# Summing GNN messages in spans of 32 nodes on quarters of TensorE's columns instead of 64 nodes on halves

## The chip, the core and the metric

The kernel runs on one core of a Trainium2 chip. The metric is the device time of one execution in microseconds (us). A core has TensorE (PE, with its weight loads shown as PEld), VectorE (DVE), ScalarE (ACT), GpSimd (POOL), SyncE (SP) and 16 DMA engines; all of them run on their own and wait for one another through semaphores.

## The reference: what is computed

The program is a stack of four blocks on 1250 nodes of 512 features, all in float32: graph attention, a mixture of 64 experts, a message-passing layer with a GRU cell, and a spline network. The edges are 20,000 edges of a random graph in both directions with 1250 self-loops, 21,250 in all, sorted by destination `dst`. The change lies in the message-passing layer:

```
m_in = concatenate([h[src], edge_attr], axis=1)          # 21250 x (512 + 128)
m    = relu(m_in @ W1.T + b1) @ W2.T + b2
agg  = segment_sum(m, dst, num_segments=1250)            # sums per destination node
gi   = agg @ W_ih.T + b_ih
gh   = h @ W_hh.T + b_hh
...                                                      # GRU cell, batch norm, h + bn
```

Since W2 is linear, the kernel sums relu(...) per node first (the tensor `rT`, features by nodes) and multiplies by W2 behind the sum.

## The kernel before

The work runs in stages: attention, routing, shared experts and experts (to about 1050 us of the trace), a stage that forms `ptab` = h @ W1[:512].T + b1 per node and writes it to HBM, the message loop (L900 to L938), and then the GRU cells and the spline network. A scheduler puts each engine's instructions into an order when the program is built: it goes by the order of the program, and an instruction that isn't ready by its estimate is passed by later ones that are. `tc.issue_after(x)` makes what is issued within it come behind x on x's engine. Within an engine the order is then fixed, and an instruction that waits holds up all behind it.

Edges are cut into 167 tiles of 128 (`ET`). As they are sorted by destination, a tile's edges lead to few nodes: about 7.5 per tile. The loop takes 8 tiles (a group) at a time, in two windows of `WT` = 4 tiles, each with 64 nodes (`WN`) around the place where its edges are expected.

- `eat` (L907): one DMA on SP's queue brings the edge features of 8 tiles, 512 KB, two buffers.
- `at` (L912): DVE writes, per tile, a 128 x 64 matrix of zeros and ones: row e, column n is 1 if edge e leads to the window's node n. It comes from `dnear`, the destination plus 1, or 0 if it isn't near the place where it is expected.
- `messages` (L885) takes a pair of tiles, one of each window: two gathers on POOL (`hg`, L203, called by L891: 128 rows of 2 KB from `ptab`, four pairs of buffers), two matmuls into `pm` (L892: 128 edges x 512), DVE's addition m = pm + hg (L894) and ACT's relu on m (L895). Behind some of them ACT's queue issues loads of later weights (`load_late`).
- `ps` (L921): for each of the two tiles a matmul with `at` as the weights: 64 columns of the array, so 64 rows of the PSUM tile `ps`. The two windows of the pair lie in its two halves. Four pairs are accumulated.
- ACT copies `ps` to `s` (L924), TensorE transposes it in four pieces to `pt` (L935), and DVE adds each window's 64 columns of it to `rT` at the window's place (L938): two additions a group.

The core of it, with the placing by window:

```
for h, i in enumerate(js):
    nc.tensor.matmul(ps[h * WN:(h + 1) * WN], at[:, i], m[:, h], start=j == 0,
                     stop=j == WT - 1 or i == n - 1)
...
for c in range(DC):
    nc.tensor.transpose(pt[:, c], s[:, c * P:(c + 1) * P], ident)
for i in range(2):
    r = rT[:, :, window(w + i):window(w + i) + WN]
    nc.vector.tensor_add(r, r, pt[:, :, i * WN:(i + 1) * WN])
```

In groups 5, 6 and 7 the node degrees are also turned into a row (`cnt`, L929 to L931). Edges that aren't near their place are counted once at the start (`far_i`); behind the loop, all engines read the count and skip a slow path (L941) if it is zero, as it is here.

Other lines that the text speaks of: L399 is the router's matmul (64 columns), L579 to L590 the shared experts, with DVE's product L583 and sum L590; L619 a comparison of 128 x 128 by DVE; L628 the load of the experts' token lists on SP and L710 the loads of the experts' weights (SP, 1.5 MB each); L682 to L691 a check of the experts' loads; L726 the experts' first matmuls, which for small experts put four tiles of 32 tokens side by side on quarters of the columns (128*32); L720, L736 and L743 the experts' transposes and second matmuls; L832 an addition of 128 x 512 by DVE; L1027 the first matmul behind the loop.

Of the kernel before, what the change touches and what calls it, by code (L numbers as in the profile page):

```python
# [10 lines left out]
F32 = mybir.dt.float32  # L11
# [3 lines left out]
I32 = mybir.dt.int32  # L15
U32 = mybir.dt.uint32
AF = mybir.ActivationFunctionType
OP = mybir.AluOpType
AX = mybir.AxisListType
# [3 lines left out]
P = 128  # L23
N = 1250
NT = 10
NP = NT * P
LAST = N - (NT - 1) * P
D = 512
# [23 lines left out]
HB = P // 2  # L52
WT, WN = 4, 64
NWIN = -(-ET // WT)


def window(w):

    return max(0, min(NP - WN, round((w + 0.5) * WT * P * N / E - WN / 2)))

# [19 lines left out]
def gnn_ffn_kernel(ctx: ExitStack, tc: tile.TileContext, a: dict, out: bass.AP):  # L80
# [57 lines left out]
    hT = const.tile([P, DC, NP], F32, name="hT")  # L138
    deg = const.tile([P, NT], F32, name="deg")

    def row(start, n):
# [452 lines left out]
    with tc.tile_pool(name="moe", bufs=1, side="right") as mw, tc.tile_pool(name="moe_w", bufs=6) as ew:  # L594
        with tc.tile_pool(name="moe_s", bufs=1) as keep, \
# [83 lines left out]


            cap = keep.tile([P, 1], F32, name="cap")
            nc.vector.tensor_scalar(cap, rank, float(TWOS), None, op0=OP.is_ge)  # L682
# [165 lines left out]
    with ExitStack() as kan:  # L848
# [11 lines left out]
        if True:  # L860
# [22 lines left out]
            nc.vector.memset(rT, 0.0)  # L883

            def messages(work, psum, parts, ahead, late=lambda i: None):  # L885

# [3 lines left out]
                for i, (t, eat_t) in enumerate(parts):  # L890
                    gather(hg[:, i], ptab, srci[:, t:t + 1])  # L891
                    nc.tensor.matmul(pm[:, i], eat_t, w1e, start=True, stop=True)  # L892
                m = work.tile([P, 2, D], F32, name="m")
# [5 lines left out]

            with tc.tile_pool(name="msg_e", bufs=3) as work, \  # L900
                    tc.tile_pool(name="msg_c", bufs=2) as chunks, \
                    tc.tile_pool(name="msg_ep", bufs=2, space=PSUM) as psum:
                for w in range(0, NWIN, 2):
                    t0 = w * WT
                    n = min(2 * WT, ET - t0)
                    eat = chunks.tile([P, 2 * WT * P], F32, name="eat")
                    nc.sync.dma_start(out=eat[:, :n * P], in_=a["edge"][:, t0 * P:(t0 + n) * P])  # L907
                    at = work.tile([P, 2 * WT, WN], F32, name="at", bufs=2)
                    for i in range(2):
                        ts = slice(i * WT, min((i + 1) * WT, n))  # L910
                        k = ts.stop - ts.start
                        nc.vector.scalar_tensor_tensor(  # L912
                            at[:, ts], iot[:, None, :WN].to_broadcast([P, k, WN]), float(window(w + i) + 1),
                            dnear[:, t0 + ts.start:t0 + ts.stop, None].to_broadcast([P, k, WN]),
                            op0=OP.add, op1=OP.is_equal)
                    ps = psum.tile([P, D], F32, name="ps", bufs=2)
                    for j in range(WT):
                        js = [i for i in (j, j + WT) if i < n]
                        m = messages(work, psum, [(t0 + i, eat[:, i * P:(i + 1) * P]) for i in js], 4, load_late)
                        for h, i in enumerate(js):  # L920
                            nc.tensor.matmul(ps[h * WN:(h + 1) * WN], at[:, i], m[:, h], start=j == 0,  # L921
                                             stop=j == WT - 1 or i == n - 1)
                    s = work.tile([P, D], F32, name="s", bufs=2)
                    nc.scalar.activation(s, ps, AF.Copy)  # L924
                    if w in (10, 12, 14):
                        c0, m = CHUNKS[w // 2 - 5]
                        pc = psum.tile([1, 512], F32, name="pt")
                        for j in range(m // P):
                            nc.tensor.matmul(pc[:, j * P:(j + 1) * P], deg[:, c0 // P + j:c0 // P + j + 1],  # L929
                                             ident, start=True, stop=True)  # L930
                        nc.scalar.activation(cnt[:, c0:c0 + m], pc[:, :m], AF.Copy)  # L931

                    pt = psum.tile([P, DC, P], F32, name="pt")
                    for c in range(DC):
                        nc.tensor.transpose(pt[:, c], s[:, c * P:(c + 1) * P], ident)  # L935
                    for i in range(2):
                        r = rT[:, :, window(w + i):window(w + i) + WN]
                        nc.vector.tensor_add(r, r, pt[:, :, i * WN:(i + 1) * WN])  # L938

            far = nc.values_load(far_i[:, :], min_val=0, max_val=P * ET)  # L940
            with tc.If(far):  # L941
                with tc.tile_pool(name="far_k", bufs=1) as keep, \
                        tc.tile_pool(name="far_w", bufs=2) as work, \
                        tc.tile_pool(name="far_q", bufs=2, space=PSUM) as psum:
                    sums = keep.tile([P, NT, D], F32, name="sums")
                    nc.vector.memset(sums, 0.0)
                    for t in range(ET):
                        eat = work.tile([P, P], F32, name="eatf")
                        nc.sync.dma_start(out=eat, in_=a["edge"][:, t * P:(t + 1) * P])
                        m = messages(work, psum, [(t, eat)], 2)[:, 0]  # L950
                        for j in range(NT):
                            at = work.tile([P, P], F32, name="at")
                            nc.vector.tensor_scalar(at, iot, float(j * P), dres[:, t:t + 1],
                                                    op0=OP.add, op1=OP.is_equal)
# [385 lines left out]
```

## Time and profile before

| | us |
|---|---|
| median of 8 runs | 1990.03 (1986.88 to 1992.84) |
| profiled execution | 1993.95, span of its instructions 1992.2 |
| granted TensorE clock, mean of the span | 0.969 of full |
| message loop, first pm (1111.49) to the first matmul behind it (1388.35) | 276.9 |

In the lines of the profile, PE is matmuls, PEld weight loads, and L912 is line 912 of the kernel. A group line has the line, engine and operation, output<-inputs by the program's names, the form (for TensorE weights as rows*columns, then the data that is streamed), the count, then busy time and mean ns of one (busy time counts what overlaps once), and then the idle time of the engine just before, with what ended it. A timeline line has start, duration, engine, line and operation; neighbours of one kind are put together (x4). Matmuls are pipelined, so the duration of one is longer than the distance to the next.

### The profile page before, as it was taken

What the parts mean: (1) busy time and instruction counts of PE and PEld (TensorE: products, weight loads), DVE (VectorE), ACT (ScalarE), POOL (GpSimd) and SP (SyncE); (2) the same over time, 40 slices, a digit from 0 to 9 for tenths busy, and PEclk for the clock granted to TensorE, in tenths of its full rate; (3) what the DMA queues carried; (4) which work ended last, traced back from release to release, by engine and by line L of the source; (5) the groups of instructions that cost most, each with busy time, mean ns of one, the idle gap of its engine ahead of it and who ended that gap; (6) DMA issues with size and microseconds to landing.
All of it is one profiled execution on the core that took longest, in us unless ns stands there. A gap on an engine that the chain in (4) does not pass through costs nothing. (4 is left out here: it accounts for less than half of the span.)

```text
span 1992.2 us, 20446 instructions
## 1 busy us (share of the span) xinstructions
PE 1861.2 (93%) x7391; PEld 896.1 (45%) x7391; DVE 1034.3 (52%) x1740; ACT 757.5 (38%) x1193; POOL 440.8 (22%) x421
## 2 busy tenths in 40 slices
PE   6999998785999999999989799998999999998989
PEld 4673232242544444444434233332446866665633
DVE  8675958263111111111137254554234988799994
ACT  3215653231012222222222134333014886787772
POOL 0000002225034444444420365663000000000000
PEclk9999999786999999999999899999999999999999
DMA  8000000002579899898962577774010000000000
GB/s 305 4 1 2 1 22 1 1 22 75 208 205 304 272 311 307 248 299 298 298 188 85 161 225 237 248 248 139 24 71 0 1 32 32 32 11 1 11 10 22
DMA packets 68257, 247.14 MB, mean 124 GB/s; under 512 B 11872, under 2 KB 14560, under 8 KB 59044
## 3 DMA queue, kind: packets, MB, share of 16 engines
q1 hardware_dynamic: 29810, 147.56, 19.7%
q0 software_dynamic: 32656, 83.97, 16.3%
q10 hardware_dynamic: 5666, 14.05, 2.0%
q8 instruction: 65, 1.06, 0.2%
q14 instruction: 60, 0.49, 0.1%
HBM read 210.15 MB, written 35.39 MB: 123 GB/s over the span
## 5 line engine op out<-in xcount | busy, mean ns | idle before, releaser
L726 PE MATMUL pg<-w,xT 128*128 128x512 f32 (+4 forms) x752 | 274.8, 595 | 2.0 <-DMA w<-in_experts 1.5
L730 DVE TENSOR_TENSOR gs<-gs,pg 128x256 f32<-128x256 f32 (+2 forms) x76 | 31.9, 420 | 388.1 <-ACT gs L729 388.1
L203 POOL DMA_INDIRECT hg<-ptab,srci x167 | 158.1, 947 | 189.9 <-DVE at L912 91.1
L726 PEld LDWEIGHTS pg<-w,xT 128*128 128x128 f32 (+4 forms) x752 | 105.4, 164 | 158.5 <-issue 156.6
L892 PE MATMUL pm<-w1e,eat 128*128 128x512 f32 x334 | 170.4, 625 | 6.6 <-DVE m L894 5.8
L749 POOL DMA_INDIRECT acc<-y,goal x94 | 140.6, 1495 | 156.2 <-ACT y L747 134.4
L743 PE MATMUL py<-w,gT 128*128 128x512 f32 (+4 forms) x376 | 149.4, 611 | 9.6 <-ACT gT L738 3.3
L894 DVE TENSOR_TENSOR m<-pm,hg 128x1024 f32<-128x1024 f32 x84 | 102.3, 1218 | 103.0 <-PE pm L892 81.9
L1176 PE MATMUL pk<-basis,w1s 128*128 128x256 f32 x640 | 150.6, 381 | 4.3 <-DVE basis L1158 4.3
L1199 PE MATMUL py<-block,basis 128*128 128x512 f32 x320 | 141.6, 603 | 9.3 <-DVE basis L1158 9.3
L481 DVE SCALAR_TENSOR_TENSOR wt<-ex,cnts 128x1024 f32<-128x1024 f32 (+1 forms) x120 | 119.7, 1039 | 51.0 <-ACT ex L479 32.7
L479 ACT ACTIVATE ex<-ps 128x1024 f32<-128x1024 f32 (+1 forms) x120 | 101.3, 882 | 109.6 <-PE ps L474 70.2
L895 ACT ACTIVATE m<-m 128x1024 f32<-128x1024 f32 x84 | 88.2, 1050 | 141.9 <-DVE m L894 121.6
L1176 PEld LDWEIGHTS pk<-basis,w1s 128*128 128x128 f32 x640 | 119.9, 190 | 42.7 <-issue 14.6
L1131 ACT ACTIVATE sq<-held,negk 128x512 f32<-128x512 f32 x180 | 127.3, 709 | 24.3 <-DVE cube L1135 24.2
L1135 DVE SCALAR_TENSOR_TENSOR cube<-held,knots,sq 128x512 f32<-128x512 f32 x180 | 134.1, 747 | 4.4 <-ACT sq L1131 4.1
L747 ACT ACTIVATE y<-py,gate 128x512 f32<-128x512 f32 (+2 forms) x76 | 52.2, 686 | 160.6 <-PE py L743 120.4
L729 ACT ACTIVATE gs<-pg 128x256 f32<-128x256 f32 (+2 forms) x76 | 29.1, 383 | 219.7 <-PE pg L726 219.7
L203 POOL DMA_INDIRECT xg<-xtab,tok x76 | 75.0, 987 | 156.3 <-PE pt L720 120.1
L892 PEld LDWEIGHTS pm<-w1e,eat 128*128 128x128 f32 x334 | 56.0, 191 | 103.5 <-issue 90.8
L1199 PEld LDWEIGHTS py<-block,basis 128*128 128x128 f32 x320 | 61.6, 194 | 86.2 <-issue 71.7
L1142 ACT ACTIVATE right<-cube 128x512 f32<-128x512 f32 x135 | 84.0, 622 | 39.9 <-DVE cube L1135 35.9
(266 smaller groups left out, 2775.3 us busy)
## 6 DMA issues: line engine op xcount, KB each, us to landing
w<-in_experts SPq DMA_DIRECT2D x64, 1536.0 KB
eat<-in_edge SPq DMA_DIRECT2D x20, 512.0 KB
acc<-zero SPq DMA_DIRECT2D x33, 256.0 KB
part<-acc SPq DMA_DIRECT2D x30, 256.0 KB
block<-in_w SPq DMA_DIRECT2D x3, 1536.0 KB
w1s<-in_w1s ACTq DMA_DIRECT2D x4, 1024.0 KB
block<-in_Wih ACTq DMA_DIRECT2D x4, 768.0 KB
block<-in_Whh ACTq DMA_DIRECT2D x4, 768.0 KB
```

What stands on the lines that cost most here:

```text
L203: nc.gpsimd.indirect_dma_start(out=dst, out_offset=None, in_=table, in_offset=IndirectOffsetOnAxis(ap=at, axis=0))
L479: nc.scalar.activation(ex[:, :, :n], p[:, :, :n], AF.Exp, scale=DK ** -0.5)
L481: nc.vector.scalar_tensor_tensor(wt[:, :, :n], ex[:, :, :n], HUGE, cnts[:, b, None, n0:n0 + n].to_broadcast([P, 2, n]), op0=OP.min, op1=OP ...
L726: nc.tensor.matmul(ph[p0:p0 + n], xT[:, c, p0:p0 + n], weights[r][:, c:2 * DC:DC], start=c == 0, stop=c == DC - 1)
L743: nc.tensor.matmul(py[p0:p0 + n], gT[:, f, p0:p0 + n], weights[r][:, k:k + 2].rearrange("p a b -> p (a b)"), start=f == 0, stop=f == 1)
L749: nc.gpsimd.indirect_dma_start(out=next(turn), out_offset=IndirectOffsetOnAxis(ap=self.goal[:n, r, h:h + 1], axis=0), in_=y[p0:p0 + n], in ...
L892: nc.tensor.matmul(pm[:, i], eat_t, w1e, start=True, stop=True)
L894: nc.vector.tensor_add(m[:, :k], pm[:, :k], hg[:, :k])
L1131: nc.scalar.activation(self.sq[k], self.x, AF.Square, bias=negk[:, k:k + 1])
L1135: nc.vector.scalar_tensor_tensor(self.cube[k], self.x, knots[:, k:k + 1], self.sq.pop(k), op0=OP.subtract, op1=OP.mult)
L1176: nc.tensor.matmul(pk[o], w[:, o * P:(o + 1) * P], b[:, c], start=half == 0 and g == 8 and c == 0, stop=half == 1 and g == 7 and c == 1)
L1199: nc.tensor.matmul(py[m], b[:, c, m * P:(m + 1) * P], w, start=g == 8 and c == 0, stop=g == 7 and c == 1)
```

## The change

Windows become shorter and narrower: `WT` = 2 tiles and `WN` = 32 nodes, four of them (`WG`) in a group of 8 tiles; there are 21 groups as before. A window no longer lies where its edges are expected but begins at the destination of its first edge (`head`). For that, all partitions get row 0 of `dst` by one DMA on SP, and DVE works out, once and ahead of the experts, for each edge its place in its window plus 1, or 0 where it has none (`inwin`), how many edges have none (`out_i`), and for each of the 128 rows of `ps` the node to which it belongs (`aim`). On these inputs the destinations within 256 neighbouring edges lie at most 17 apart.

In the loop, a step now takes four tiles, one of each window: two calls of `messages` as before, and then four matmuls of 32 columns, into the four quarters of `ps`. The sums of a step are held back until the next step's pm matmuls are issued, and the copy of `ps` and what follows it too. The rows of `ps` are no longer at fixed nodes, and two windows can have the same node, so the transposes become true matmuls with a matrix of zeros and ones, `to` (row p, column n is 1 if row p of `ps` belongs to node n of the group's 128), which transposes, places and adds up in one; DVE then adds 128 columns to `rT` in one instruction. DVE writes `to` once a group and `at` in one instruction instead of two; `at` has three buffers instead of two, m four instead of three. The slow path tests `out_i`. `dres` and `far_i` are still used by the attention stage.

```diff
-WT, WN = 4, 64
-NWIN = -(-ET // WT)
+WT, WN, WG = 2, 32, 4
+NGRP = -(-ET // (WT * WG))
...
+            head_i = keep.tile([P, ET], I32, name="head_i")
+            d0 = a["dst"]
+            nc.sync.dma_start(out=head_i,
+                              in_=bass.AP(tensor=d0.tensor, offset=d0.offset, ap=[[0, P], [1, ET]]))
+            head = keep.tile([P, NGRP, WG], F32, name="head")
+            nc.vector.tensor_copy(head.rearrange("p g q -> p (g q)"), head_i[:, ::WT])
...
+            nc.vector.memset(inwin, -1.0)
+            nc.vector.tensor_sub(inwin[:, :whole], dstf[:, :whole * WT].rearrange("p (w i) -> p w i", i=WT),
+                                 heads[:, :whole, None].to_broadcast([P, whole, WT]))
...
+            nc.vector.tensor_scalar(ok, flat[:, :ET], 0.0, None, op0=OP.is_ge)
+            nc.vector.scalar_tensor_tensor(ok, flat[:, :ET], float(WN), ok, op0=OP.is_lt, op1=OP.mult)
+            nc.vector.scalar_tensor_tensor(ok, dnear, 0.0, ok, op0=OP.is_gt, op1=OP.mult)
+            nc.vector.scalar_tensor_tensor(flat[:, :ET], flat[:, :ET], 1.0, ok, op0=OP.add, op1=OP.mult)
+            inside = keep.tile([P, 1], F32, name="inside")
+            nc.vector.tensor_reduce(inside, ok, AX.X, OP.add)
+            po = psum.tile([1, 1], F32, name="pt", bufs=3)
+            nc.tensor.matmul(po, inside, ones[:, 0:1], start=True, stop=True)
+            nc.vector.tensor_scalar(out_i, po, -1.0, float(P * ET), op0=OP.mult, op1=OP.add)
+            nc.vector.tensor_scalar(aim, head[:, :, 0], qf, None, op0=OP.add)
+            for q in range(1, WG):
...
+                nc.vector.scalar_tensor_tensor(aim, step, over, aim, op0=OP.mult, op1=OP.add)
...
-            with tc.tile_pool(name="msg_e", bufs=3) as work, \
+            with tc.tile_pool(name="msg_e", bufs=4) as work, \
...
+                def summed(j, n, ps, at, sums):
+                    with tc.issue_after(firsts[-1].ins):
+                        for q, m in sums:
+                            i = q * WT + j
+                            nc.tensor.matmul(ps[q * WN:(q + 1) * WN], at[:, i], m, start=j == 0,
                                              stop=j == WT - 1 or i == n - 1)
+                def placed(g, ps, to):
                     s = work.tile([P, D], F32, name="s", bufs=2)
                     nc.scalar.activation(s, ps, AF.Copy)
...
                     for c in range(DC):
-                        nc.tensor.transpose(pt[:, c], s[:, c * P:(c + 1) * P], ident)
-                    for i in range(2):
-                        r = rT[:, :, window(w + i):window(w + i) + WN]
-                        nc.vector.tensor_add(r, r, pt[:, :, i * WN:(i + 1) * WN])
+                        nc.tensor.matmul(pt[:, c], s[:, c * P:(c + 1) * P], to, start=True, stop=True)
+                    r = rT[:, :, span(g):span(g) + P]
+                    nc.vector.tensor_add(r, r, pt)
+                held = []
+                for g in range(NGRP):
...
+                    to = work.tile([P, P], F32, name="to", bufs=3)
+                    nc.vector.tensor_scalar(to, iot, float(span(g)), aim[:, g:g + 1], op0=OP.add,
+                                            op1=OP.is_equal)
+                    ps = psum.tile([P, D], F32, name="ps", bufs=2)
+                    for j in range(WT):
+                        sums = []
+                        for q0 in range(0, WG, 2):
+                            qs = [q for q in (q0, q0 + 1) if q * WT + j < n]
+                            m = messages(work, psum, [(t0 + q * WT + j, eat[:, (q * WT + j) * P:][:, :P])
+                                                      for q in qs], 4, load_late)
+                            sums += [(q, m[:, i]) for i, q in enumerate(qs)]
+                        for todo in held:
+                            todo()
+                        held = [lambda g=g, j=j, n=n, ps=ps, at=at, sums=sums: summed(j, n, ps, at, sums)]
+                    held.append(lambda g=g, ps=ps, to=to: placed(g, ps, to))
...
-            far = nc.values_load(far_i[:, :], min_val=0, max_val=P * ET)
+            far = nc.values_load(out_i[:, :], min_val=0, max_val=P * ET)
```

`firsts` is the list of all pm matmuls in the order of the program; `messages` appends to it.

## The prediction

> **What bounds it now.** All times are in us. I read four views. The engine shares and the windows give the stage and its limit, the groups by form give the size of each part, and the timeline of TensorE gives the price of one step. The first line of the page's engine shares names the engine; the windows then take three stretches from inside the message loop.
>
> ```profile
> PE 1861.2 (93%) x7391; PEld 896.1 (45%) x7391; DVE 1034.3 (52%) x1740; ACT 757.5 (38%) x1193; POOL 440.8 (22%) x421
> ```
>
> ```profile
> 1220.00:1260.00 40.00, 40.00 (x123) 12.94 (x124) 20.55 (x26) 15.45 (x17) 25.20 (x28) 1.00 0.79 256
> 1260.00:1300.00 40.00, 40.00 (x120) 12.56 (x118) 21.30 (x26) 15.19 (x16) 25.23 (x27) 1.00 0.77 244
> 1300.00:1340.00 40.00, 40.00 (x123) 13.02 (x121) 22.43 (x30) 15.68 (x17) 24.64 (x27) 1.00 0.80 256
> ```
>
> The columns are PE, PEld, DVE, ACT, POOL busy, granted clock, DMA share, GB/s. In this loop TensorE never stops, at full clock; DVE is at 54%, ACT at 39%, POOL at 63%, DMA at 0.79. So time taken off TensorE here comes off the end until the next of these is full. The loop runs from the first pm (1111.49) to the first GRU matmul (1388.35): 276.9. The groups by form say what fills it:
>
> ```profile
> L892 PE MATMUL pm<-w1e,eat 128*128 128x512 f32 x334 | 170.4, 625 | 6.6 <-DVE m L894 5.8 <-DVE pv L839 0.8
> L203 POOL DMA_INDIRECT hg<-ptab,srci x167 | 158.1, 947 | 189.9 <-DVE at L912 91.1 <-DVE m L894 53.7 <-issue 43.1
> L921 PE MATMUL ps<-m,at 128*64 128x512 f32 x334 | 92.4, 632 | 0.4 <-ACT m L895 0.4
> L935 PE MATMUL pt<-ident,s 128*128 128x128 f32 x84 | 13.3, 282 | 5.0 <-issue 3.6 <-ACT s L924 1.4
> L726 PE MATMUL pg<-w,xT 128*32 128x512 f32 x128 | 14.6, 595 | 0.0
> ```
>
> An f32 matmul is recorded twice (334 records for 167 tiles): two passes. Two 64-column sums already run side by side: 167 take 92.4, 0.55 each, though one record lasts 0.63. The last line, from the experts, shows the form that the change brings: 64 quarter-wide matmuls in 14.6, 0.23 each, so four at once do run in the time of one. TensorE's timeline gives one period of the loop (8 tiles):
>
> ```profile
> 1264.72 0.60 PE L935 MATMUL pt<-ident,s 128*128 128x128 f32 x4
> 1265.15 1.02 PE L892 MATMUL pm<-w1e,eat 128*128 128x512 f32 x2
> 1266.11 1.08 PE L921 MATMUL ps<-m,at 128*64 128x512 f32 x4
> 1267.12 1.98 PE L892 MATMUL pm<-w1e,eat 128*128 128x512 f32 x4
> 1269.03 1.08 PE L921 MATMUL ps<-m,at 128*64 128x512 f32 x4
> ...
> 1275.89 1.13 PE L892 MATMUL pm<-w1e,eat 128*128 128x512 f32 x2
> 1276.85 0.60 PE L935 MATMUL pt<-ident,s 128*128 128x128 f32 x4
> ```
>
> From transposes to transposes is 12.13. One pair of tiles, sums to sums, is 2.92 (1266.11 to 1269.03). Passes in an unbroken run start 0.43 apart, so two pm are 1.72 and the sums with both changes of shape 1.20: 0.86 streaming and 0.34 for going to half-width columns and back. Four pairs are 11.68; the transposes are the other 0.45.
>
> **The change, part by part.**
>
> *Sums.* Four pairs of halves become two quartets a group. The price of a quartet is read in the experts: wide passes begin at 891.49, quarters at 893.40, the next transposes at 896.98. Four wide passes and four quartets take 5.49 against 1.72 + 3.43 streaming, so going in and out costs 0.34 there too, and a quartet 0.86. A step of four tiles is then 4 x 0.86 + 0.86 + 0.34 = 4.63, against 2 x 2.92 = 5.84: 1.21 off, 2.42 a group.
>
> *Merging.* The four transposes (0.45) become four true matmuls of 128 columns with `to`: eight passes. No row has this form. From below: the router's matmuls (L399, 64 columns) load 25 weights in 2.87, 0.115 a pass, 0.92 in all. From above: 256-column passes (the shared experts' last chunk) start 0.216 apart, 1.73 in all. 128 columns at the streaming rate would be 0.107, below the loading rate, so I take the lower row, 0.95. They keep pm's full-width shape. The group loses 0.50 here.
>
> The Trainium skill ("TensorE: Matmul & The Clock Gate", Terms) says that transpose mode is four times as fast for f32, which speaks against this part: four times 0.45 is 1.80 a group, an estimate from that page, and the saving would be about 18 smaller. The trace shows two records per f32 matmul against one per transpose, so I stay with the rows.
>
> A group becomes 12.13 - 2.42 + 0.50 = 10.21; 167 tiles are 20.9 groups, so 1.92 x 20.9 = **40** come off.
>
> *What is late next.* POOL: a gather is 0.945 and at least 0.30 between two, 8 x 1.25 = 10.0 a group, 208.7 for 167, against TensorE's 213. It just fits, but with hardly any slack: today POOL waits for DVE's m (0.73 or 1.17 before each first gather of a pair). I take **2** off the gain for it. DVE: 4 x 1.22 (m), 0.69 (rT in one addition, priced by L832), 0.44 (`at`), 0.28 (`to`, by L619) are 6.3 of 10.2. ACT: 4 x 1.06 and 0.60 are 4.8. DMA: gathers 43.8 MB, edges 10.9, late weights 7.3 are 62 MB in some 225, 275 GB/s; at 256 the share was 0.80, so 0.86.
>
> The Trainium skill ("TensorEngine Tiling (Array Packing)", PSUM Bottleneck) warns that tiling makes TensorE faster and not the emptying of PSUM. Here that would bind only past 10.2 a group; DVE's 6.3 says it doesn't.
>
> *Holding back.* Sums wait until the next step's pm are issued (`issue_after`). A step's second pm is followed by 3.4 of pm before its sums; DVE 1.22 and ACT 1.06 fit in that. Four m buffers hold two steps. Nothing is lost there. `placed` needs ACT's copy s (0.60) after the last sums: today the gap is filled by one pm (1275.89 above), and I assume that again.
>
> *Preparation before the experts.* About 24 DVE instructions: three on 167 elements at 0.32 (L120), some more at 0.24 to 0.33, thirteen small ones at 0.15: 4.6 in all; one DMA on SP (`head_i`, ahead of the experts' weights), and two passes. TensorE is busy 10.00 of each 10.00 from 500 to 540 while DVE does 0.9 to 2.7, so the shared experts hide it; without that cover it costs 4.6. The added wait is DVE's for head_i; behind it stand the shared experts' products (L583), for which TensorE waits. At 498.29 such a wait for a DMA (11.28 on DVE) cost TensorE 2.63. Between -2.6 (if the order there becomes better) and 4.6 I take **1**.
>
> The two far paths test a count that is zero for edges in order as here; the stage behind the loop is unchanged and moves up. Sum: 40 - 2 - 1 = 37. The profiled execution took 1993.95 (span 1992.2 and 1.75 around it): 1957. That execution is 3.9 above the median of the runs shown, 1990.03; on the median, **1953**.
>
> **Rivals.**
> 1. *Part of the gain goes into the merge.* At the upper row the eight passes cost 17 more (0.78 x 21); if nothing fills the wait for s, 0.75 a group (0.60 and a semaphore) is 16. Either gives 1970, both 1986. For it: the form isn't in the trace. Against: the filling of today.
> 2. *Gathers or DMA become the bound.* If the loop gets no more than 256 GB/s, 62 MB take 243, and with 3.2 ahead of the first gather and 8.5 behind the last pm 254: 1968. Against: 361 to 426 GB/s at 500 to 520.
> 3. *Slower: the merge stalls TensorE each time.* It decides if the merge follows its sums directly in TensorE's queue and ACT takes the copy behind the second relu of the next step. Then s comes 1.22 + 1.06 + 0.60 and semaphores behind that pm, some 3.1, of which the sums cover 0.86: 2.25 x 21 = 47, more than the 37: 2000. Against: a free pm can be issued there.
> 4. *The quarters don't run together*, because other matmuls come between them: 2.57 more a step, 108: 2061. Against: they are issued in one loop, as the experts' are.
>
> **Numbers.** Main case 0.63 (1944 to 1963: merge at 0.92 and the preparation at -2.6 below; preparation in full and some POOL waits above). Rival 1 0.18, rival 2 0.08, no gain for a mix of these 0.03, rival 3 0.06, rival 4 0.02. The range takes in the singles of rivals 1 and 2: 1944 to 1974. Faster by over 0.2% (4, about what a measurement here can tell) 0.89, within 0.03, slower 0.08.
>
> **What would show it.** Right: TensorE at 40.00 of 40.00 in the loop, steps of 4.6 between quartets, a group of 10.2, sums near 40 busy in all, idle before gathers near 0.30. Merge: eight passes in about 0.95, or 1.7 (rival 1). Wrong: idle before the merge by ACT s (1, 3), DVE m waiting for gathers (2), sums over 90 (4), TensorE idle between 470 and 550 (preparation). I am wrong above all if TensorE stops being full in the loop.

## The result, and the profile after

The changed kernel takes **1998.4** us (median of 11 runs, 1993.0 to 2000.7), the kernel before 1989.9 beside it: a ratio of **1.0041** [1.0031, 1.0051] (in brackets here and below the 95% interval), slower by 0.4%. 1953.0 was predicted. The profiled execution took 2001.7, span 2000.0. Three executions that took over 2% longer than the others of their program in the same session (one of `e4_whole_deg`, and one of the kernel before beside each of `e14_whole_deg_2` and `e16_reversed_deg_2`) are left out of all times.

The span falls into three parts, cut at the first pm and at the first GRU matmul. The last two rows are later runs of the same two programs (`e9_before_again`, `e5_changed_again`, below), each in another session, that is, a set of runs made together on one chip; they belong here because they change what there is to explain.

| | first pm at | loop | behind it | span |
|---|---|---|---|---|
| before, first profile | 1111.5 | 276.9 | 603.9 | 1992.2 |
| changed, first profile | 1113.2 | 285.3 | 601.5 | 2000.0 |
| before, later session | 1078.5 | 269.9 | 603.5 | 1952.0 |
| changed, later session | 1081.4 | 240.7 | 601.9 | 1923.9 |

So there are two kinds of session. In the first, the kernel before takes 1990 us and the change costs 0.4%; in the second, before takes 1953 and the same change gains 1.6% (0.9844 [0.9828, 0.9861]). Which kind a session was could not be chosen, and the chip numbers 0 and 1 occur in both kinds.

In the first profile of the change, the windows in the loop, with the columns of the prediction (PE, PEld, DVE, ACT, POOL busy, clock, DMA share, GB/s):

```profile
1220.00:1260.00 40.00, 34.64 (x129) 14.70 (x130) 18.20 (x22) 15.54 (x18) 24.53 (x27) 0.96 0.74 230
1260.00:1300.00 40.00, 35.49 (x123) 14.21 (x122) 17.90 (x21) 13.91 (x15) 22.75 (x25) 0.92 0.71 237
1300.00:1340.00 40.00, 37.41 (x127) 14.53 (x127) 19.69 (x23) 15.08 (x16) 25.46 (x27) 0.95 0.75 247
```

TensorE is no longer full (34.64 to 37.41 of 40.00), and in these stretches its clock is lower too (0.92 to 0.96 instead of 1.00). The groups by form say what it waits for; the last line is of the kernel before, for the addition to rT:

```profile
L932 PE MATMUL pm<-w1e,eat 128*128 128x512 f32 x334 | 166.3, 637 | 31.0 <-DVE m L934 29.3 <-issue 0.8 <-DVE pv L877 0.8
L947 PE MATMUL ps<-m,at 128*32 128x512 f32 x334 | 53.1, 609 | 0.6 <-ACT m L935 0.6
L963 PE MATMUL pt<-to,s 128*128 128x128 f32 x168 | 29.3, 330 | 9.2 <-ACT s L953 8.0 <-issue 1.1
L965 DVE TENSOR_TENSOR rT<-rT,pt 128x512 f32<-128x512 f32 x21 | 14.4, 688 | 71.4 <-PE ps L947 29.2 <-PE pt L963 24.2 <-PE pm L932 15.9
```

```profile
L938 DVE TENSOR_TENSOR rT<-rT,pt 128x256 f32<-128x256 f32 x42 | 17.7, 421 | 16.4 <-PE pt L935 12.2 <-issue 2.1 <-PE pm L892 1.3
```

The sums fell from 92.4 to 53.1, as meant. But TensorE now stands idle 31.0 before pm (6.6 before), 29.3 of it (5.8 before) until DVE's m, and DVE, which has far less to do than TensorE, stands 71.4 before its addition to rT (16.4 before), waiting for TensorE. Each seems to wait for the other. The timelines of TensorE, DVE and POOL at one such place follow; L963 is the merge, the four products with `to`:

```profile
1261.49 1.04 PE L947 MATMUL ps<-m,at 128*32 128x512 f32 x2
1262.47 1.16 PE L963 MATMUL pt<-to,s 128*128 128x128 f32 x8
1263.55 1.06 PE L947 MATMUL ps<-m,at 128*32 128x512 f32 x6
1264.54 3.70 PE L932 MATMUL pm<-w1e,eat 128*128 128x512 f32 x8
1268.17 1.07 PE L947 MATMUL ps<-m,at 128*32 128x512 f32 x8
1271.42 1.13 PE L932 MATMUL pm<-w1e,eat 128*128 128x512 f32 x2 [2.18 <-DVE m L934]
```

```profile
1261.76 1.22 DVE L934 TENSOR_TENSOR m<-pm,hg 128x1024 f32<-128x1024 f32 x1 [0.60 <-PE pm L932]
1269.35 0.69 DVE L965 TENSOR_TENSOR rT<-rT,pt 128x512 f32<-128x512 f32 x1 [6.37 <-PE ps L947]
```

```profile
1252.18 0.95 POOL L206 DMA_INDIRECT hg<-ptab,srci  x1 [1.21 <-DVE m L934]
...
1264.71 0.95 POOL L206 DMA_INDIRECT hg<-ptab,srci  x1 [0.30 <-issue]
1265.96 0.95 POOL L206 DMA_INDIRECT hg<-ptab,srci  x1 [0.30 <-issue]
1271.64 0.94 POOL L206 DMA_INDIRECT hg<-ptab,srci  x1 [4.72 <-DVE m L934]
```

The merge ends at 1263.6, yet DVE's addition, which needs nothing else that is late, starts at 1269.35. TensorE tells the others that a matmul is done by adding one to a semaphore; this increment is called its signal below. In the trace's record of this semaphore, the increments of the merge and of the three signals that follow it stand together at 1269.3 to 1269.6: the merge's completion signal came 5.7 us **late**. DVE goes through its list in order, so m, the relu, the gathers and the next pm waited behind the addition. Two things stand out. The merge lies *between* one quarter (x2) and the other three (x6), an order that the scheduler chose when the program was built; such a split stands in 7 of the 21 groups. And POOL had issued twelve gathers 0.30 apart without a pause, then stopped, and the signals came 2.4 after its last one ended.

### The profile page after: what moved, and what is told of

It reads as the page before. It is cut to its first block, busy times and chain, and to the rows that moved or that the text cites. A ratio compares the mean times of both kernels' runs of the same rounds, so it can differ in the third digit from the quotient of the medians.

```text
span 2000.0 us, 20622 instructions
## 1 busy us (share of the span) xinstructions
PE 1841.2 (92%) x7477; PEld 909.3 (45%) x7477; DVE 1029.5 (51%) x1742; ACT 757.1 (38%) x1193; POOL 442.0 (22%) x421
## 5 line engine op out<-in xcount | busy, mean ns | idle before, releaser
L932 PE MATMUL pm<-w1e,eat 128*128 128x512 f32 x334 | 166.3, 637 | 31.0 <-DVE m L934 29.3
L932 PEld LDWEIGHTS pm<-w1e,eat 128*128 128x128 f32 x334 | 62.8, 202 | 124.7 <-issue 82.2
```

The source lines that it names most:

```text
L932: firsts.append(nc.tensor.matmul(pm[:, i], eat_t, w1e, start=True, stop=True))
```

## Experiments

### First theory: a merge between quarters makes signals late

> The changed kernel, with nothing but the order on TensorE altered: the four quarters of a step are issued from the last to the first (so the first one already waits for the later m, and the four start together), the copy of s is issued right after its sums, and the merge, with the three groups' degree matmuls, is issued behind the next step's whole quartet instead of wherever the builder put it. Theory (split quartets): in every second group the merge stood between one quarter and the other three, TensorE's completion signals then came 5.3 to 5.7 us late, and DVE's addition to rT, everything behind it, and the clock paid for it. Then the loop goes from 285 to 235-250 us, no merge's signal is more than 1 us late, and the time is 1948-1965. Rival 1 (the merge or the wait for s is simply dearer than forecast, wherever it stands): the loop stays above 275, time 1985 or more. Rival 2 (the gathers on POOL bound the group near 13 us once TensorE is faster): the loop stays above 275 and pm waits for m because m waits for a gather, 1985 or more.

> As e1_whole, and the ten degree matmuls (one column wide) and their three copies are issued ahead of the loop instead of in groups 5 to 7. If one-column matmuls too are followed by late completion signals (the trace of before shows DVE and ACT waiting until 1213.24 in that stretch), this is 3 to 12 us less than e1_whole. Rival: the degree matmuls cost only their own passes (10 at under 0.1 us); then it is within 1.5 us of e1_whole.

> The changed kernel with windows of 4 tiles and 64 nodes, two to a group, instead of 2 tiles and 32 nodes, four to a group: holding the sums back, the merge with its 128x128 matrix, the preparation and the far path all stay as in the change; only the sums run on halves of the columns, as before the change. Theory (split quartets): here the merge nowhere stands between two halves of a pair, so no signal is late; the sums cost what they did before (about 4.8 us a group), the merge some 0.6 more than the transposes, so the loop is 277 + 21 x 0.6 = 285 to 295 with TensorE full, and the time 1998-2010, the cause of the loop's length being another one than in the change. Rival (holding back, or the merge itself, makes the stalls): then the same stalls come on top of the dearer sums, loop 310 or more, 2025 or more.

> The kernel before, with one thing forced: the four transposes of a group are issued between the two halves of the next group's first pair, in every group. Theory (split): completion signals come some us late after each, DVE's additions to rT and the m additions behind them wait, TensorE runs idle and its clock falls: 2040 or more. Rival (a split only costs what the engine itself shows): the two halves of one pair no longer run together, one pass of 0.86 and one drain of 0.34 more in each group, 21 x 1.2 = +25, so about 2005-2018, and no late signal.

The edits, in this order:

```
# e1_whole
-    for q, m in sums:
+    for q, m in sums[::-1]:
...
+    with tc.issue_after(last.ins):       # the last sum of the next step
         nc.tensor.matmul(pt[:, c], s[:, c * P:(c + 1) * P], to, start=True, stop=True)
# e4_whole_deg: and the loop over CHUNKS that makes cnt stands ahead of the groups
# e2_halves
-WT, WN, WG = 2, 32, 4
+WT, WN, WG = 4, 64, 2
# e3_split_before: in the kernel before, half 0 of a group's first pair, the last group's
# four transposes, half 1, each behind the other by issue_after
```

| | time | ratio to before | loop |
|---|---|---|---|
| e1_whole | 1916.8 | 0.9813 [0.9797, 0.9830] | 230.7 |
| e4_whole_deg | 1917.1 | 0.9814 [0.9794, 0.9833] | 226.7 |
| e2_halves | 1964.0 | 1.0046 [1.0030, 1.0063] | 279.2 |
| e3_split_before | 1975.5 | 1.0105 [1.0088, 1.0121] | 292.1 |

Before took 1954.0 here. The ratio of `e1_whole` is nearly the predicted one (1953.0 / 1990.0 = 0.9814), and it seemed to prove the theory, though time and loop lie below the ranges expected of it. `e4_whole_deg` gains nothing over it: its loop is 4.0 shorter, but with the degree matmuls ahead of the loop the first pm comes 4.1 later (1085.5 against 1081.4). But `e3_split_before` shows no late signal at all behind its 20 splits; it lost what its rival said, 1.1 us a group (22.2 of loop over `e9_before_again`) for one more pass and one more change of shape. And `e2_halves` has no stalls either: its loop, below the 285 to 295 expected, is 9.3 over that of `e9_before_again`, about the 0.45 a group by which the merge is dearer than the transposes. And before was 36 us shorter than it had been. So the chip, or the session, had to be ruled out.

### The same programs again

> The changed kernel as it is, on the chip that runs the next three. e1_whole ran on a chip on which the kernel before takes 1954 us and not 1990, so the late signals could belong to the first chip and not to the order. Theory (split quartets): the order is fixed by the build, so the late signals come again behind the same seven splits, the loop is over 275 us, and the ratio to before is 1.00 to 1.01. Rival (that chip's): no signal late, loop under 250 us, ratio under 0.99.

> The kernel before as it is, to have its trace from another chip. In the first runs (before 1990.0, changed 1998.4) TensorE's completion signals came late in both kernels; in e1_whole and e5_changed_again, on chips where before takes 1954, not one of 1089 did, and the change gained 1.6%. Theory (late signals belong to the first chip and cost the change more than the kernel before): on a chip of the 1954 kind the loop of before is 267 to 272 us (against 276.9 with late signals), its group 12.1 us, its stages ahead of the loop 28-31 us shorter than in the first profile, and the change's loop (240.7) is 27 to 32 less. Rival (the first chip is slower in another way, a lower clock all over): the loop stays near 277 and the 36 us are spread over the whole span.

> The changed kernel with one edit: the quarters of a step are issued from the last to the first, so that the first one already waits for the step's later m. The builder then puts every merge beside pm's and none between two quarters. Theory (split quartets): as e1_whole without its placed merges, loop 228 to 245 us, ratio to before 0.98 to 0.986. Rival (it was the place of the merge behind the next step in e1_whole, which gives s a step more to be copied, that helped): the loop stays above 260, ratio above 0.995.

```
# e6_reversed: the changed kernel and this alone
-    for q, m in sums:
+    for q, m in sums[::-1]:
```

The first theory, that this order by itself makes signals late, falls with `e5_changed_again`: 1924.3, ratio 0.9844, loop 240.7, TensorE full. At the same place in its trace the order is the same, and DVE starts 0.04 after the merge (its idle time before all its additions to rT is 22.5 instead of 71.4):

```profile
1206.09 1.04 PE L947 MATMUL ps<-m,at 128*32 128x512 f32 x2
1207.06 1.16 PE L963 MATMUL pt<-to,s 128*128 128x128 f32 x8
1208.15 1.06 PE L947 MATMUL ps<-m,at 128*32 128x512 f32 x6
```

```profile
1208.26 0.69 DVE L965 TENSOR_TENSOR rT<-rT,pt 128x512 f32<-128x512 f32 x1 [0.58 <-PE pt L963]
```

```profile
1220.00:1260.00 40.00, 40.00 (x149) 15.89 (x149) 22.38 (x27) 17.51 (x19) 28.55 (x31) 1.00 0.85 287
```

Not one of its 1089 signals is late, nor one in the other traces of such sessions. `e9_before_again` tells the same of the kernel before: its loop is 269.9, not 276.9, and its stages ahead of the loop are 33.0 shorter; the rest is equal within 0.4, so the first session is not slower all over. The late signals of the first session lie in a few places, the same ones in both kernels ahead of the loop. One is the router's, far from the change: in the first profile of before, in that of the changed kernel, and then in `e5_changed_again`:

```profile
454.99 3.67 PE L399 MATMUL ps<-rw,hT 128*128 128x64 f32 x16
469.71 0.29 DVE L402 TENSOR_TENSOR pr<-ps,rb 128x128 f32<-128x128 f32 x1 [17.34 <-remote]
```

```profile
455.42 3.67 PE L402 MATMUL ps<-rw,hT 128*128 128x64 f32 x16
467.71 0.29 DVE L405 TENSOR_TENSOR pr<-ps,rb 128x128 f32<-128x128 f32 x1 [12.56 <-remote]
```

```profile
435.22 3.68 PE L402 MATMUL ps<-rw,hT 128*128 128x64 f32 x16
438.94 0.29 DVE L405 TENSOR_TENSOR pr<-ps,rb 128x128 f32<-128x128 f32 x1 [3.99 <-PE ps L402]
```

11.0 and 8.6 us against 0.04, with no quarter near it. In the changed kernel's first profile it came 2.7 behind the end of a series of 24 gathers on POOL (to 465.0).

`e6_reversed` (1917.4, 0.9813 [0.9796, 0.9829], loop 233.4) gives the other result: with one token changed no merge stands between quarters, and 7.2 us of loop are gone, 1.03 for each of the 7 splits.

### What a split costs by itself

> As e4_whole_deg (group of 10.15 us, loop 226.7), with the quarters in their old order and the merge forced between the first quarter and the other three, in every group. If such a split is what makes signals late, each group shows a merge whose signal comes 4 us late or more, and loses 4 to 7 us to it: loop 310 to 370. If a split only costs what TensorE itself does (one pass of 0.86 and one switch of 0.34 more, as the 1.14 a group in e3_split_before): group 11.3, loop 250, no late signal.

> As e7_split13, with the group's four transposes of s (as the kernel before has them) in place of the merge's four products, so that what stands in the split is no true product; rT is then not the merged sum. If any full-width instruction between quarters makes signals late: as e7_split13, 310 to 370 less 0.5 a group. If it takes the merge's products (two passes each, s as weights): no late signal here, loop about 240, and late ones in e7_split13.

> As e7_split13 (merge forced inside every group's first step, loop 247.8, 1.05 us a group over e4_whole_deg), with the merge between two quarters and the other two. If a split costs one more pass and one more switch wherever it stands: loop 246 to 249. If the lone quarter is what costs: under 238. On a chip where signals come late (before at 1990), this one shows whether every split draws a late signal: 20 of them, loop over 300; or whether they come at moments that don't depend on splits.

```
# e7_split13, on e4_whole_deg with the old order of quarters
     for k, (q, m) in enumerate(sums):
+        if between and k == 1:
+            last = between(last)         # the last group's merge
# e8_split13_tr: nc.tensor.transpose(pt[:, c], s[...], ident) in place of the merge's products
# e13_split22: k == 2
```

All three are single executions. `e7_split13`: loop 247.8, which is 21.1 over `e4_whole_deg` for 20 splits: 1.05 each; in the middle of the loop a group takes 11.31 (from the merge at 1119.17 to that at 1130.48), 1.16 more. `e8_split13_tr`: 237.0, the transposes some 0.5 a group cheaper than the products. No late signal in either. `e13_split22` met a session of the first kind (1994.5, before 1994.2): loop 276.6, but only behind 4 of its 20 split merges did DVE's addition start more than 4 us late. Splits don't draw late signals one by one.

### How much a late signal costs

> The changed kernel with one more instruction on DVE ahead of the addition to rT in the six groups 3, 9, 11, 13, 15 and 17 (those whose signals came 5.3 to 5.7 us late in the first profile): a copy of about 5 us that waits for the merge, as a late signal would make DVE wait. If late signals of that size, six of them, are what the first chip took from the loop, and there is no slack behind them, the loop grows by 20 to 35 us (240.7 to 261-276), TensorE's clock shows a half-speed stretch behind each, and pm waits for m. If messages running ahead hide most of a late signal: under 10 us.

> The kernel before with the copy of 5.5 us on DVE that e10_delay has, ahead of the additions to rT in the same six groups. e10_delay lost 14.1 us of loop to six such copies (240.7 to 254.8), 2.4 of 5.5 each. If the change is not more sensitive to a late signal than the kernel before, and the first chip's 45 us against 7 came from more or longer late signals, this loop too grows by 10 to 18 us, from 269.95 to 280-288. If holding the sums back made the loop more sensitive: under 5 us here, 270-275.

```
+    if g in (3, 9, 11, 13, 15, 17):      # in before: w // 2
+        nc.vector.tensor_copy(idle, pt.rearrange("p c f -> p (c f)")[:, None, :].to_broadcast([P, 10, DC * P]))
     nc.vector.tensor_add(r, r, pt)
```

Both are single executions. `e10_delay`, without late signals: six copies of 5.49 made the loop 14.1 longer (254.8), 2.4 each; the expectation was 20 to 35, or under 10, a miss of both. The messages that run ahead hide more than half of such a wait. So these six waits reproduce 14.1 of the 44.7 that the changed loop lost in the first session. There DVE's addition came over 1 us late behind eight merges, and the first merge alone ended 8.1 later behind the first pm (36.05 against 27.96 in `e5_changed_again`); the rest of the 44.7 has not been separated. `e11_before_delay` fell on a session of the first kind (2028.4, before 1994.2). Its loop is 312.4, 35.5 over the first profile of before: 5.9 for each copy, all of it, again outside both expected ranges. The trace shows no new late signals that would explain it: in the loop ACT's longest waits for finished sums are 4.6, 1.1 and 1.1 (3.6, 1.1 and 1.1 in the first profile of before), and behind the transposes DVE never starts more than 0.9 late. So, as far as two executions in sessions of different kinds can tell, holding the sums back made the loop less sensitive to a wait of DVE, not more.

### No split, in a session with late signals

> As e6_reversed (quarters from the last to the first), and the degree matmuls ahead of the loop. On a chip of the 1954 kind: 1915 to 1919, loop 226 to 231. On a chip with late signals, where before takes 1990: if splits and one-column matmuls draw them, there are fewer than half as many late signals in the loop as in the first profile of the changed kernel, and the time is 1950 to 1970; if late signals come whatever the order, 1985 or more.

> e4_whole_deg again (whole quartets, merge behind them, degree matmuls ahead of the loop; 0.981 of before where no signal is late), for a session in which signals come late (before near 1990). If merges between quarters and one-column matmuls are what draws late signals: at most 3 late ones in its loop, loop 227-240, ratio 0.977 to 0.986. If quarters draw them in any order: 10 or more late, loop 255-280, ratio 0.99 to 1.003. In a session without late signals: 0.981 once more.

> e2_halves again (holding back, merge and preparation of the change, sums on halves; loop 279.25 where no signal is late), for a session in which signals come late. If quarters draw them: as the kernel before, it loses 5 to 12 us, loop 284-292. If the merge's products or holding back draw them: 30 us or more, loop 310 or more. In a session without late signals: 279 once more.

> e12_reversed_deg, timed. In a session with late signals (before near 1990): if splits and one-column matmuls draw them, loop 228-240 and ratio 0.977 to 0.986; if quarters draw them in any order, loop 255-280 and ratio 0.99 to 1.003. In a session without: 0.981, as e6_reversed, with which it shares all but the place of the ten degree matmuls.

```
# e12_reversed_deg, e16_reversed_deg_2: e6_reversed, and the loop that makes cnt ahead of the groups
# e14_whole_deg_2 and e15_halves_2 are e4_whole_deg and e2_halves
```

The first three met sessions without late signals: 1915.9 (`e12_reversed_deg`, a single execution); 1915.2, ratio 0.9808 [0.9790, 0.9826] (`e14_whole_deg_2`); 1967.4 (`e15_halves_2`, a single execution). `e16_reversed_deg_2` met one with them, and it decides against splits and degree matmuls as the cause: 2004.3, ratio 1.0063 [1.0045, 1.0081], loop 284.0 (beyond both expected ranges) against 227.8 for the same program in `e12_reversed_deg`. With no split and no degree matmul in the loop, eight merges have their signal 5.3 to 5.8 late. TensorE, DVE and POOL in it:

```profile
1261.45 1.06 PE L947 MATMUL ps<-m,at 128*32 128x512 f32 x8
1262.45 1.16 PE L956 MATMUL pt<-to,s 128*128 128x128 f32 x8
```

```profile
1269.35 0.69 DVE L958 TENSOR_TENSOR rT<-rT,pt 128x512 f32<-128x512 f32 x1 [5.91 <-PE ps L947]
```

```profile
1265.93 0.95 POOL L206 DMA_INDIRECT hg<-ptab,srci  x1 [0.30 <-issue]
1271.63 0.95 POOL L206 DMA_INDIRECT hg<-ptab,srci  x1 [4.76 <-DVE m L934]
```

It is the picture of the changed kernel without the split, and again the signals (1269.3 to 1269.5) come 2.45 behind POOL's last gather, with POOL standing still. In both traces the eight large releases in the loop (three or four increments at once) lie 2.1 to 2.5 behind the end of a gather that ended an unbroken series, and POOL does not begin again until 1.6 to 2.3 after them. Single late increments also come while a series still runs (six in the loop of the changed kernel), so the tie is not perfect.

This gives the second theory: **in these sessions TensorE's signals are held back while POOL issues gathers without a pause.** It can be counted in all traces. A series is a run of gathers (all of POOL's indirect DMAs) less than 0.36 apart; each of TensorE's signals from 300 us on is put down by how many gathers of the running series had begun when its matmul ended (a series counts for 2.5 behind its last gather). "Not on time" is a signal without a recorded increment within 0.25 of that end. About half of these have no recorded increment at all (164 are missing from the five traces), so the column counts late and unrecorded signals together.

| gathers of the series so far | five traces with late signals: signals, not on time | four without: signals, not on time |
|---|---|---|
| no series | 1755, 0 | 1361, 0 |
| 1 to 3 | 1871, 87 (5%) | 1546, 0 |
| 4 to 6 | 181, 71 (39%) | 99, 0 |
| 7 to 9 | 95, 53 (56%) | 55, 0 |
| 10 to 12 | 94, 77 (82%) | 50, 0 |
| 13 and more | 38, 32 (84%) | 117, 0 |

(The five: before, changed, `e11_before_delay`, `e13_split22`, `e16_reversed_deg_2`; the four: `e9_before_again`, `e5_changed_again`, `e4_whole_deg`, `e2_halves`; in the other traces without late signals every signal is on time too.) Two more counts do not rest on the record of increments. Of the 105 merges (in before, transposes) in the loops of the five traces, 19 end at the seventh or a later gather of a series, and behind 18 of these DVE's addition starts over 1 us later than the merge and DVE's own work allow; of the other 86 it does so behind 4. In the four traces without late signals it is none of 84, 26 of them at the seventh gather or later. And held against `e9_before_again` instruction by instruction, the first profile of before falls behind by 21.6 between 341 and 372, by 11 between 429 and 476 and by 5.6 between 1027 and 1143; everywhere else the distance changes by less than 2: POOL's longest series in it are two of 24 (from 332 and 436), one of 12 (from 481) and one of 18 (from 1115), all others have 6 or fewer.

A full TensorE alone is not enough to draw late signals: it is full in the loop of before too (40.00 of 40.00 in the windows of the prediction), in the same kind of session, and that loop lost 6.9.

And this is what the change does to POOL. In the first profile of before, every second gather waits for DVE:

```profile
1267.77 0.94 POOL L203 DMA_INDIRECT hg<-ptab,srci  x1 [1.17 <-DVE m L894]
1269.02 0.95 POOL L203 DMA_INDIRECT hg<-ptab,srci  x1 [0.30 <-issue]
1270.69 0.94 POOL L203 DMA_INDIRECT hg<-ptab,srci  x1 [0.73 <-DVE m L894]
```

Its series are pairs (59 of 68 in the loop), and the gathers of the loop wait 53.7 in all for DVE's m. With the change, where no signal is late (`e5_changed_again`), that wait is 19.2:

```profile
L206 POOL DMA_INDIRECT hg<-ptab,srci x167 | 158.4, 949 | 155.6 <-DVE at L974 91.3 <-issue 38.1 <-DVE m L934 19.2
```

TensorE is so fast that POOL has few pauses left: 8 of 20 series have 12 gathers or more there, and 9 of 20 in the first profile of the change. So the long series come from the change and not from the late signals. Where signals are held, POOL runs until no hg buffer is free, because DVE's m does not come; then it stops, the signals come, and it all starts again, every 25 to 26 us.

> As e4_whole_deg (whole quartets, degree matmuls ahead of the loop), with the merge between the second and the third pm of the step after next, so that it touches no sums on either side. In a session with late signals (before near 1990): if merges that touch a quartet draw them, at most 4 merges late in the loop, loop 228-245, ratio 0.978 to 0.988. If late signals come whatever the neighbours (TensorE full is enough): loop 265-290, ratio 0.995 to 1.007. In a session without: loop 225-229, ratio 0.981, as e4_whole_deg.

> e17_between again, for a session with late signals (before near 1990). If merges that touch a quartet draw them: at most 4 merges late in the loop, loop 228-245, ratio 0.978 to 0.988. If they come whatever the neighbours: loop 265-290, ratio 0.995 to 1.007. In a session without: 0.981 once more, and the question stays open.

```
# on e4_whole_deg: the merge between the step's two calls of messages
+    if q0 and waiting:
+        behind, waiting = waiting(firsts[-1]), None
...
+    with tc.issue_after(behind.ins) if behind else ExitStack():
         firsts.append(nc.tensor.matmul(pm[:, i], eat_t, w1e, start=True, stop=True))
```

Both met sessions without late signals: 1917.0 and 1915.9, 0.9814 [0.9793, 0.9836] and 0.9809 [0.9792, 0.9825]. They say nothing of their question, whether the merge's neighbours matter. The count above needs no such rule: in `e16_reversed_deg_2` seven of the eight late merges end at the tenth gather of a series, and the eighth behind gathers whose pauses were 0.40 and 0.41.

**What stays open.** The tie of late signals to POOL's series is shown by counting and by the moments of release, not by an edit: none of the kernels that met such a session had POOL's pauses put back into the changed loop (fewer hg buffers would do it). Why some sessions hold signals and others don't, the traces don't show; in the others a series of 50 gathers (`e4_whole_deg`) or 70 (`e14_whole_deg_2`) holds none. One more difference is on record: in the five traces increments of ACT and DVE are missing too (32 of 1133 and 79 of 1645 in before), nearly all during POOL's series, where the other traces miss three at most. These engines' signals were not late, but a cause that disturbs the recording, or a part that the recording itself has in the delay, is a rival that no run here tests.

## Why the prediction was wrong

**The step that failed** is "What is late next", POOL: "It just fits, but with hardly any slack: today POOL waits for DVE's m", for which "I take **2** off the gain". The pauses were seen in the profile, that they would go was foreseen, and they were priced as POOL's own time alone. With them went the premise that "time taken off TensorE here comes off the end". In the sessions of the kind in which the result was measured, TensorE's signals came late where POOL had no pauses, and DVE's addition, m and the next pm waited for them: the loop of the change lost 44.7 (285.35 against 240.67), that of before 6.9. That is 37.8 more, against a gain of 29.3 where no signal is late. The lateness and its price are measured; that the missing pauses bring it on rests on the counts above. So "I am wrong above all if TensorE stops being full in the loop" is what happened, by a wait that none of the four rivals names. Rival 3 lies near the measured time (2000), but by chance: it put 47 on the wait for ACT's s, and the merge waits 8.0 in all for it in the first profile of the change and 0.7 in `e5_changed_again`.

A sign stood in the profile of before: the router's matmuls end at 458.7, and DVE's addition that needs nothing else starts at 469.71, behind 24 gathers without a pause. And the forecast was subtracted from a time, 1990, in which such waits already had about 40 us.

The other steps are best read where no signal is late:

- *Sums*: a step of 4.63. `e4_whole_deg` has 4.62 (1218.55 to 1223.17 below), and a group is 10.15 against 10.21 forecast. The sums are busy 44.7 there, against "near 40", and 52.5 in `e5_changed_again` with its splits.

```profile
1213.03 1.06 PE L947 MATMUL ps<-m,at 128*32 128x512 f32 x8
1214.02 1.16 PE L960 MATMUL pt<-to,s 128*128 128x128 f32 x8
1215.02 3.60 PE L932 MATMUL pm<-w1e,eat 128*128 128x512 f32 x8
1218.55 1.06 PE L947 MATMUL ps<-m,at 128*32 128x512 f32 x8
1219.54 3.70 PE L932 MATMUL pm<-w1e,eat 128*128 128x512 f32 x8
1223.17 1.06 PE L947 MATMUL ps<-m,at 128*32 128x512 f32 x8
```

- *Merging*: 0.95. From quartet to quartet with the merge it is 5.52, without 4.62: 0.90. The dearer merge was sized from the rows rightly. By the Trainium skill ("TensorE: Matmul & The Clock Gate", Terms), which calls transpose mode four times as fast for f32, four times 0.45, an estimate of 1.80, was possible; the measurement is half of that.
- *Quartets whole*. Against rival 4 the prediction said that the quarters "are issued in one loop". The loop in the program does not keep them together: the scheduler put the merge between them in 7 groups, 7.2 in all (`e6_reversed`). That is most of what the change misses of its forecast in such sessions: 28.9 gained (1953.2 to 1924.3) of 37. With whole quartets the same session gives 35.8 (1953.2 to 1917.4).
- *Gap before the merge filled by a pm*: right, 0.7 of idle time by ACT s in `e5_changed_again`.
- *Preparation*: 1 forecast; the first pm comes 1.7 later in the first pair of profiles, 2.9 in the second. Behind the loop 1.7 to 2.4 are gained, which was not forecast.
- *DMA* (rival 2): in `e5_changed_again` 282 to 287 GB/s at a share of 0.85 to 0.87, where 275 at 0.86 were forecast; no bound.

## What to carry to other kernels

An engine's short pauses in the profile may be doing work for others; before a change takes them away, ask which waits end in them, and price the loss at that place and not as the engine's own time. A consumer that starts 11 us after its only late input ended is worth a question before anything is forecast. A time that differs by 2% between sessions for the same program is a reason to run both kernels again before the cause is sought in the code: the first theory here fitted one trace in every detail and fell with the second. Matmuls that are to run side by side on parts of the columns stay together only if the order says so: make the first of them wait for the last one's input, or tie them with an explicit order.

## What the runs showed of the hardware that was not expected

- In the first profiles and in two of the eight later sessions, TensorE's completion signals came up to 11 us late (the router's in the first profile of before, 458.7 to 469.7) while POOL issued gathers 0.30 apart. Of ACT's recorded increments none was late, of DVE's 1645 in before at most 6, though some of both are missing from the record. Both kernels run 32 to 33 us longer ahead of the loop in the first session.
- A full-width matmul between two column parts of one step costs one more pass and one more change of shape: 1.05 to 1.16 with quarters (`e7_split13`), 1.1 with halves (`e3_split_before`).
- Four f32 products of 128 x 128 cost 0.90 (`e4_whole_deg`), two recorded passes each, against 0.45 for four f32 transposes (before).
